# A conditioned block on one core: zero matmuls early, bias rows on another queue, and the first slot tile ahead of the second in the opening

## The chip, the core and the metric

The kernel runs on one NeuronCore of a Trainium2 chip. The core has five engines with a queue of instructions each: TensorE (PE: matmuls; its weight loads are listed apart as PEld), VectorE (DVE), ScalarE (ACT), GpSimd (POOL) and SyncE (SP), which here only starts DMAs. Sixteen DMA engines move data between HBM and SBUF, the on-chip memory; matmul results go to PSUM banks. The metric is the device time of one execution in microseconds; lower is better. The median of three runs before the change is 463.99 us.

## What is computed

`x` holds 32 sequences of 128 tokens with 512 features, all float32. `cond` holds one row of 512 per sequence, and `mask` says for each token whether it takes part in the first half of the block (for these inputs, only a minority of the tokens, at the ends of the sequences).

```python
emb = silu(t) @ ada_w + ada_b
shift, scale, gate_msa = split(emb, 3, axis=1)
norm = layernorm(x) * (1.0 + scale[:, None]) + shift[:, None]
norm = where(m, norm, 0.0)
fwd = gelu(norm @ ssm_w1 + ssm_b1) @ ssm_w2 + ssm_b2
bwd = flip(gelu(flip(norm) @ bwd_w1 + bwd_b1) @ bwd_w2 + bwd_b2)
x = x + gate_msa[:, None] * where(m, fwd + bwd, 0.0)
ff_ada = silu(t) @ ffada_w + ffada_b
shift_mlp, scale_mlp, gate_mlp = split(ff_ada, 3, axis=1)
ff_norm = layernorm(x) * (1.0 + scale_mlp[:, None]) + shift_mlp[:, None]
h = gelu_tanh(ff_norm @ ff_w1 + ff_b1)
return x + gate_mlp[:, None] * (h @ ff_w2 + ff_b2)
```

Nothing mixes tokens of a sequence, so the first half of the block has to be done only for tokens that the mask keeps.

## The kernel before

**First half: slots.** The kept tokens are packed into at most 512 slots, four tiles (0 to 3) of 128 slots; a loop at the end, not entered here, takes any remainder. The opening works out which token sits in each slot. The mask is loaded on ACT's queue (L110), counted and transposed (L427 to L441, PE result `pb`), cumulated (`pg`, L449), and combined with the slot numbers (`pick_slots`, L213). `find_slots(h)` makes, for two slot tiles at a time, one matrix product (`pl_s`, L225) and three DVE operations that end in the token indices `token_i_s`. `gather_slots` (L254) has POOL issue two indirect DMAs that fetch these rows of `x` into `xc`.

**Conditioning.** SP loads `ada_w` into `ada_a` in four blocks of rows for shift and scale (`load_ada`, L124) and one block with all rows of the gate's columns (L146). `silu(cond)` is transposed to `sT` (L460 to L466). `modulation` (L275) multiplies `sT` with `ada_a` into PSUM (`pm_ss` for shift and scale, `pm_g` for the gate, one strip of 32 output rows each) and DVE adds the bias rows `modb_a` to give `mod1`. `slot_part` (L288) turns rows of `mod1`, one per sequence, into rows per slot by a product with the 0/1 matrix `pick`. The bias rows come through `broadcast_rows` on POOL's queue (L423), three DMAs; three more on POOL's queue (L477 to L481) fetch `bias_rows`, the biases of the hidden layers.

**Slot tiles 0 and 1.** `statistics` takes both tiles at once: mean and variance of each on DVE, then one reciprocal root for both on POOL. `modulated` applies two DVE operations per tile; PE transposes each tile (`transposed_slots`, L175) into a PSUM bank and ACT copies it to `xT_s`, 256 columns for the two tiles. `hidden` (L182) then computes, for each of eight blocks f of the hidden layer, four matmuls with 256 columns into one bank (`ph_s`) and a Gelu on ACT. `project` (L196) multiplies back (`po_s`), and `finish_slots` (L296) adds the bias, multiplies by the gate, adds `xc` and stores the rows to a DRAM buffer `x1_rows`.

**Weights and queues.** SP's queue carries, in this order, the conditioning, then `w1` and `w2` (the first half's weights, in four loads), `fw1`, the conditioning of the second half `ada_f`, small bias rows, `fw2`, and the `x` of the second half. `load_behind_gathers` (L134) puts a one-element POOL memset into the target of each of the four `w` loads, so that SP issues them only after POOL has issued the gathers written ahead of them.

**Around them.** The order of the instructions on all engines is the order of the program, written out by hand (`manual_schedule`, L361). Between the first-half products, DVE also builds sums of blocks of the second half's weights (`combine`, L313, and `weight_sums`, L568), once `fw1` has landed. When tiles 0 and 1 are stored, POOL gathers their rows into the second half's `x` (`take_first_half`, L670, one indirect DMA per sequence); statistics and normalisation follow on DVE (L704 to L721), and PE transposes the result of the second group of sequences (L734) between the products of slot tile 3 (L1193). The second half runs after that, in four pairs of token groups, with block products in the manner of Strassen (`a_m`, `e_m`, L906; `a_o`, `e_o`, L1093).

**PSUM.** There are eight banks in three pools: `ps_t` (2, transposes), `ps_h` (3, hidden products), `ps_o` (3, the others). A new tile of a pool takes the bank of the oldest one and waits until its readers are done.

Of the kernel before, what the change touches and what calls it, by code (L numbers as in the profile page):

```python
# [22 lines left out]
def kernel(  # L23
# [90 lines left out]
    def broadcast_rows(t, vec, queue):  # L114

        n = vec.shape[0] // D
        each = t.shape[0] // n
        for j in range(n):
            queue.dma_start(
                t[j * each : (j + 1) * each, :],  # L120
                vec[ts(j, D)].rearrange("(o d) -> o d", o=1).to_broadcast([each, D]),
            )

    def load_ada(w, which, split):  # L124

        t = adap.tile([P, KC, 3 * D], F32, tag="ada", name=f"ada_{which}")
        for k in range(KC):
            nc.sync.dma_start(t[:, k, :split], w[ts(k, P), :split])
        return t
# [4 lines left out]
    def load_behind_gathers(t, w):  # L134
        nc.gpsimd.memset(t[0:1, 0, 0:1], 0.0)
        load_blocks(t, w)
# [7 lines left out]
    w2 = ssm.tile([P, HC, D], F32, name="w2")  # L144
    ada_a = load_ada(ada_w, "a", 2 * D)
# [227 lines left out]

    upper = ssm.tile([B, 2, 4, B], BF16, name="upper")
# [48 lines left out]
    broadcast_rows(modb_a, ada_b, nc.gpsimd)  # L423
    half = const.tile([P, G], F32, name="half")
    nc.vector.memset(half, -0.5)

# [20 lines left out]
    nc.vector.tensor_copy(maskT, pb[:, :B])  # L447
    pg = ps_t.tile([P, 512], F32, tag="tr", name="pg")
# [20 lines left out]

    token_i = find_slots(0)  # L470
    gather_slots(token_i)

    load_behind_gathers(w1[:, :, :D], ssm_w1)
    load_behind_gathers(w1[:, :, D:], bwd_w1)
    load_behind_gathers(w2[:, :KC], ssm_w2)
    load_behind_gathers(w2[:, KC:], bwd_w2)
    for key, vec in (("ssm1", ssm_b1), ("bwd1", bwd_b1), ("ff1", ff_b1)):  # L477
        n = vec.shape[0] // P
        nc.gpsimd.dma_start(
            bias_rows[col[key] : col[key] + n, :], vec.rearrange("(c p) -> c p", p=P)  # L480
        )  # L481
    pick_slots(1)
# [9 lines left out]
    modulation(pm, mod1, ada_a, modb_a, 0, 2)  # L492
    gather_slots(find_slots(1, (ps_h, "h")))
    rows = [(slot_part(c, 1, ps_o, "o"), slot_part(c, 0, ps_h, "h")) for c in range(2)]
    pm = ps_o.tile([P, 512], F32, tag="o", name="pm_g")
    xT_s = ssm.tile([P, KC, NH], F32, tag="xT", name="xT_s0", bufs=2)
    xT_t = ssm.tile([P, KC, NH], F32, tag="xT", name="xT_s1", bufs=2)
    xn = group_of_tiles("s")
    mv, rstd = statistics(xc[:2], "s01")
    xn_s = [  # L500
        modulated(
            xc[c], *rows[c], f"s{c}", xn[:, c], (mv[:, c, 0:1], rstd[:, c : c + 1])
        )
        for c in range(2)
    ]
    modulation_matmuls(pm, ada_a, 2, 3, range(KC))
# [13 lines left out]
    x_of = {0: load_x(0)}  # L520
    transposed_slots(xn_s[0], xT_s[:, :, ts(0, P)], "s0")
    transposed_slots(xn_s[1], xT_s[:, :, ts(1, P)], "s1")
# [6 lines left out]
    modulation_rows(pm, mod1, modb_a, 2, 3)  # L529

# [81 lines left out]
    for c in range(2):  # L612
        h1 += hidden(xT_s, NH, w1, 0, AF.Gelu, "s0", ssm, range(4 * c, 4 * c + 3))
        if c == 0:
            total, start_at, more_i, col_l = count_more()
        gs.append(keep_gate(c, slot_part(c, 2, ps_o, "o")))
        rows = slot_part(2 + c, 1, ps_o, "o"), slot_part(2 + c, 0, ps_o, "o")
        xn_s.append(modulated(xc[2 + c], *rows, f"s{2 + c}", xn[:, 2 + c]))
        if c == 0:
            Weights(fw1, KC // 2, FF // 2, t_1).combine(0, 1, 2, 3)  # L620
        h1 += hidden(xT_s, NH, w1, 0, AF.Gelu, "s0", ssm, range(4 * c + 3, 4 * c + 4))
        if c == 1:
            transposed_slots(xn_s[0], xT_t[:, :, ts(0, P)], "s2")
# [856 lines left out]
```

## Time and profile before

The profiled execution is one run; its span, from the first to the last instruction, is 463.6 us. The three timed runs gave 462.65, 463.99 and 466.23 us.

| | |
|---|---|
| median of three runs | 463.99 us |
| span of the profiled execution | 463.6 us |
| PE busy | 448.9 us (97%) |
| DVE busy | 330.6 us (71%) |
| first dense product (`ph_s`) starts | 20.93 us |
| bytes moved, HBM read and written | 56.83 and 13.17 MB |

How to read the profile. Times count from the start of the span, in microseconds. A row of the timeline gives the start, the length, the engine, the source line, the operation, output <- input, and how often it stands there in a row; in brackets stands how long the engine had been idle before it, and what ended that. A name with q (SPq, ACTq) is the queue that starts DMAs. PE's matmuls overlap each other: one f32 matmul of 256 columns is listed with 379 ns, but the next one starts 216 ns after it, and each f32 product appears as two instructions. A wait is put down to the event that came last. The landing of a DMA is not a row; it is seen in what waited for it, or in the list of DMAs, which gives the time from issue to landing.

### The profile page before, as it was taken

To read this page: it belongs to the slowest core of one execution; us is meant where nothing else is said; L and a number is where in the kernel's file an instruction comes from. 1 tells how busy PE (TensorE), PEld (TensorE's weight loads), DVE (VectorE), ACT (ScalarE), POOL (GpSimd) and SP (SyncE) were. 2 spreads that over 40 slices of the span, in tenths; PEclk is the share of its full clock that TensorE was granted. 3 is DMA by queue.
4 is the path that set the end of the run, shared out by engine and by line. 5 is a ranking of instruction groups with operands and counts; after the bars stand their busy time and mean duration, and the time that the engine had idled before them with its cause. 6 is when DMAs were issued, how large, how long until landed. Compare 5 with 4: busy or idle time off the path is not lost.

```text
span 463.6 us, 5827 instructions
## 1 busy us (share of the span) xinstructions
PE 448.9 (97%) x2000; PEld 364.4 (79%) x2000; DVE 330.6 (71%) x538; ACT 175.7 (38%) x380; POOL 159.8 (34%) x153
## 2 busy tenths in 40 slices
PE   6899999998999999999999999999999999999995
PEld 2475385676788888888888888888888887888884
DVE  4649778998669739996787498957963985433645
ACT  3122021743355271344455514454355144552000
POOL 6200082038981000489700005987000026560000
PEclk9999999999999999999999999999999999999998
DMA  8999836693206653923077259321872432213022
GB/s 280 386 408 364 322 107 95 219 326 104 85 5 211 97 102 105 354 90 113 1 229 113 68 169 310 99 81 34 212 105 60 155 142 79 81 74 109 0 81 105
DMA packets 82419, 70.42 MB, mean 152 GB/s; under 512 B 63168, under 2 KB 63696, under 8 KB 81362
## 3 DMA queue, kind: packets, MB, share of 16 engines
q1 hardware_dynamic: 67298, 57.03, 39.4%
q0 software_dynamic: 4480, 11.66, 7.2%
q10 hardware_dynamic: 10608, 1.32, 2.0%
q8 instruction: 17, 0.28, 0.3%
q14 instruction: 16, 0.13, 0.1%
HBM read 56.83 MB, written 13.17 MB: 151 GB/s over the span
## 4 chain that ended last, share of the span: by engine, by line
PE 72%; DVE 8%; DMA 5%; SPq 4%; POOL 4%; issue 3%; ACT 3%; POOLq 0%; ACTq 0%; DVEq 0%
PE a_o L1093 17%; PE a_m L906 14%; PE e_o L1093 13%; PE e_m L906 11%; PE ph_s L188 6%; PE po_s L203 6%; SPq L745 4%; DMA x<-in_x_dram 2%; POOL x L674 1%; DMA xc<-in_x_dram,token_i_s 1%; DMA tw<-t_rows 1%; ACT xT L728 1%; PE part_s L283 1%; POOL ha L957 1%; PE pm_f L263 1%
## 5 line engine op out<-in xcount | busy, mean ns | idle before, releaser
L957 POOL TENSOR_TENSOR ha<-p_m,ha 128x512 f32<-128x512 f32 x20 | 26.2, 1311 | 151.9 <-ACT ha L964 142.0
L1093 PE MATMUL e_o<-fw,ha 128*128 128x256 f32 x256 | 57.9, 379 | 0.0
L728 ACT ACTIVATE xT<-xT,modT 128x128 f32<-128x128 f32 x112 | 44.0, 480 | 31.9 <-DMA xT<-xn 31.9
L1093 PE MATMUL a_o<-t,hb 128*128 128x256 f32 x240 | 54.1, 379 | 0.0
L1093 PEld LDWEIGHTS e_o<-fw,ha 128*128 128x128 f32 x256 | 48.6, 190 | 6.6
L1093 PEld LDWEIGHTS a_o<-t,hb 128*128 128x128 f32 x240 | 45.6, 190 | 6.2
L674 POOL DMA_INDIRECT x<-x_rows,slot_i x32 | 38.1, 1192 | 30.1 <-DMA x_rows<-t_s 18.0
L868 ACT ACTIVATE hb<-hb,biasT 128x256 f32<-128x256 f32 x64 | 29.0, 500 | 29.1 <-POOL hb L990 19.3
L957 POOL TENSOR_TENSOR hb<-p_m,hb 128x512 f32<-128x512 f32 x20 | 29.3, 1464 | 18.9 <-DVE sx L835 18.6
L920 ACT COPY p_m<-e_m 128x512 f32<-128x512 f32 x27 | 15.8, 586 | 47.9 <-PE e_m L906 47.9
L964 ACT COPY ha<-e_m 128x512 f32<-128x512 f32 x32 | 18.5, 578 | 28.6 <-PE e_m L906 26.6
L931 DVE TENSOR_TENSOR e_m<-a_m,ha 128x512 f32<-128x512 f32 x20 | 14.0, 698 | 21.6 <-POOL ha L957 9.5
L188 PE MATMUL ph_s<-xT_s,w 128*128 128x256 f32 x128 | 28.6, 381 | 0.5 <-issue 0.5
L1093 PE MATMUL a_o<-t,s 128*128 128x256 f32 x128 | 28.9, 379 | 0.0
L1093 PE MATMUL a_o<-fw,ha 128*128 128x256 f32 x128 | 28.9, 379 | 0.0
L1093 PE MATMUL e_o<-fw,s 128*128 128x256 f32 x128 | 28.9, 379 | 0.0
L203 PE MATMUL po_s<-w,h_s 128*128 128x512 f32 x64 | 28.6, 592 | 0.0
L188 PEld LDWEIGHTS ph_s<-xT_s,w 128*128 128x128 f32 x128 | 24.0, 190 | 5.2 <-ACT h_s L192 1.5
L1093 PEld LDWEIGHTS a_o<-t,s 128*128 128x128 f32 x128 | 24.3, 190 | 3.3
L1093 PEld LDWEIGHTS e_o<-fw,s 128*128 128x128 f32 x128 | 24.3, 190 | 3.3
L1093 PEld LDWEIGHTS a_o<-fw,ha 128*128 128x128 f32 x128 | 24.3, 190 | 3.3
L868 ACT ACTIVATE ha<-e_m,biasT 128x256 f32<-128x256 f32 x48 | 20.1, 468 | 16.2 <-PE e_m L906 10.5
(210 smaller groups left out, 870.0 us busy)
## 6 DMA issues: line engine op xcount, KB each, us to landing
tw<-t_rows SPq DMA_DIRECT2D x16, 896.0 KB, 5.5
x<-in_x_dram SPq DMA_DIRECT2D x16, 512.0 KB, 6.8
gate<-gate_rows POOLq DMA_DIRECT2D x8, 1024.0 KB, 5.2
out_dram<-x SPq DMA_DIRECT2D x15, 512.0 KB, 3.3
xT<-xn SPq DMA_DIRECT2D x92, 64.0 KB, 2.4
fw<-in_L_cond_ff_w_dram SPq DMA_DIRECT2D x2, 2048.0 KB, 10.5
ada_f<-in_L_cond_ffada_w_dram SPq DMA_DIRECT2D x4, 768.0 KB, 16.7
ada_a<-in_L_cond_ada_w_dram SPq DMA_DIRECT2D x4, 512.0 KB, 6.7
```

The costliest lines, as they stand in the source:

```text
L188: nc.tensor.matmul(ph[:, :n], w[:, k, ts(f, P)], xT[:, k, :], start=(k == 0), stop=(k == KC - 1))
L203: nc.tensor.matmul(po, h[f][:, ts(i, P)], w[:, f, :], start=(f == 0), stop=(f == HC - 1))
L674: nc.gpsimd.indirect_dma_start(out=xs[i // G][i % G // 2][:, i % 2], out_offset=None, in_=x1_rows[:slots, :], in_offset=bass.IndirectOffse ...
L728: nc.scalar.activation(out, src, AF.Identity, bias=shift, scale=scale)
L745: queues[b % len(queues)].dma_start(dst[ts(q, R), b], src[ts(b, R), q])
L868: nc.scalar.activation(dst[:, n], src[:, n], AF.Gelu_apprx_tanh, bias=biasT[:, f : f + 1])
L906: nc.tensor.matmul(bank[:, ts(n, QT)], self.w_block(j, product)[:, ts(n, P)], self.x_block(j, product), start=(product in ("P1", "P5") and ...
L920: nc.scalar.copy(p5, e)
L931: nc.vector.tensor_tensor(e, a, p5, add)
L957: nc.gpsimd.tensor_tensor(self.place(RESULT[j], c), self.p5[j], other, ALU.add)
L964: nc.scalar.copy(self.place(RESULT[j], c), src)
L1093: nc.tensor.matmul(part, src[:, k, ts(i, P)], w[product][:, k, :], start=(last and k == 0), stop=True, skip_group_check=True,)
```

## The change

It touches only the opening.

1. A tile of zeros in bf16 is made first on DVE, and `keep_busy(n)` issues n matmuls of 64 columns on it into a bank that nobody reads: 36 ahead of the mask's first transpose, 4 after the products of `pb`, and 8 ahead of the first `pl_s`.
2. `modb_a` is loaded on ACT's queue, directly after the mask, instead of POOL's; `bias_rows` too, after ACT's second table load.
3. `pl_s` for slot tiles 2 and 3 stands between the second and the third block of `pm_ss` on PE, and its gathers are issued ahead of the last three `w` loads (before, all four loads came between the two pairs of gathers).
4. Each of tiles 0 and 1 has its own statistics and root. PE transposes tile 0, multiplies two blocks f with its 128 columns, transposes tile 1, multiplies a third block with tile 0's columns, and then the three blocks with tile 1's columns (`hidden_of_tile`). A bank `ph_s` collects the two halves, and one Gelu takes both. Blocks 3 to 7 are as before.
5. The gate's product `pm_g` goes to four strips of 32 rows, one per block of the sum, in place of a sum in one strip. ACT copies them to SBUF (`gate_parts`), and one more product with a 0/1 matrix `strips` (made on DVE from the identity) adds the four into `pm_gate`.

On each engine the instructions after the opening are the same, in the same order.

```diff
+    broadcast_rows(modb_a, ada_b, nc.scalar)
     ada_a = load_ada(ada_w, "a", 2 * D)
     load_blocks(ada_a[:, :, 2 * D :], ada_w[:, 2 * D :])
...
+    zeros = ssm.tile([P, P // 2], BF16, name="zeros")
+    nc.vector.memset(zeros, 0.0)
+    idle = ps_h.tile([P, 512], F32, tag="h", name="idle")
+
+    def keep_busy(n):
+
+        for _ in range(n):
+            nc.tensor.matmul(idle[: P // 2, : P // 2], zeros, zeros, start=True, stop=True)
+
+    keep_busy(36)
...
-    broadcast_rows(modb_a, ada_b, nc.gpsimd)
...
+    strips = ssm.tile([P, B], F32, name="strips")
+    nc.vector.tensor_reduce(
+        strips, ident.rearrange("p (a b) -> p b a", b=B), axis=AX.X, op=ALU.add
+    )
...
+    keep_busy(4)
     pg = ps_t.tile([P, 512], F32, tag="tr", name="pg")
...
-    token_i = find_slots(0)
-    gather_slots(token_i)
-
-    load_behind_gathers(w1[:, :, :D], ssm_w1)
-    load_behind_gathers(w1[:, :, D:], bwd_w1)
-    load_behind_gathers(w2[:, :KC], ssm_w2)
-    load_behind_gathers(w2[:, KC:], bwd_w2)
     for key, vec in (("ssm1", ssm_b1), ("bwd1", bwd_b1), ("ff1", ff_b1)):
         n = vec.shape[0] // P
-        nc.gpsimd.dma_start(
+        nc.scalar.dma_start(
             bias_rows[col[key] : col[key] + n, :], vec.rearrange("(c p) -> c p", p=P)
         )
+
+    keep_busy(8)
+    gather_slots(find_slots(0))
+    load_behind_gathers(w1[:, :, :D], ssm_w1)
     pick_slots(1)
...
-    modulation(pm, mod1, ada_a, modb_a, 0, 2)
+    modulation_matmuls(pm, ada_a, 0, 2, range(KC // 2))
     gather_slots(find_slots(1, (ps_h, "h")))
-    rows = [(slot_part(c, 1, ps_o, "o"), slot_part(c, 0, ps_h, "h")) for c in range(2)]
+    load_behind_gathers(w1[:, :, D:], bwd_w1)
+    load_behind_gathers(w2[:, :KC], ssm_w2)
+    load_behind_gathers(w2[:, KC:], bwd_w2)
+    modulation_matmuls(pm, ada_a, 0, 2, range(KC // 2, KC))
+    modulation_rows(pm, mod1, modb_a, 0, 2)
+    rows = [(slot_part(c, 1, ps_o, "o"), slot_part(c, 0, *((ps_o, "o"), (ps_h, "h"))[c])) for c in range(2)]
+    gate_parts = tp.tile([P, D], F32, tag="t", name="gate_parts")
     pm = ps_o.tile([P, 512], F32, tag="o", name="pm_g")
+    for k in range(KC):
+        nc.tensor.matmul(
+            pm[ts(k, B), :], sT[:, k, :], ada_a[:, k, ts(2, D)], start=True, stop=True
+        )
+    nc.scalar.copy(gate_parts, pm)
...
-    mv, rstd = statistics(xc[:2], "s01")
-    xn_s = [
-        modulated(
-            xc[c], *rows[c], f"s{c}", xn[:, c], (mv[:, c, 0:1], rstd[:, c : c + 1])
-        )
-        for c in range(2)
-    ]
-    modulation_matmuls(pm, ada_a, 2, 3, range(KC))
+    xn_s = [modulated(xc[c], *rows[c], f"s{c}", xn[:, c]) for c in range(2)]
...
+    def hidden_of_tile(f, c):
+
+        if c == 0:
+            ph_s[f] = ps_h.tile([P, 512], F32, tag="h", name=f"ph_s0_{f}")
+        for k in range(KC):
+            nc.tensor.matmul(
+                ph_s[f][:, ts(c, P)],
+                w1[:, k, ts(f, P)],
+                xT_s[:, k, ts(c, P)],
+                start=(c == 0 and k == 0),
+                stop=(k == KC - 1),
+                skip_group_check=True,
+            )
+
     transposed_slots(xn_s[0], xT_s[:, :, ts(0, P)], "s0")
-    transposed_slots(xn_s[1], xT_s[:, :, ts(1, P)], "s1")
+    pm = ps_o.tile([P, 512], F32, tag="o", name="pm_gate")
+    nc.tensor.matmul(pm[ts(2, B), :], strips, gate_parts, start=True, stop=True)
     ptr = ps_t.tile([P, 512], F32, tag="tr", name="ptr_b")
...
     modulation_rows(pm, mod1, modb_a, 2, 3)
+    for f in range(2):
+        hidden_of_tile(f, 0)
+    transposed_slots(xn_s[1], xT_s[:, :, ts(1, P)], "s1")
+    hidden_of_tile(2, 0)
...
     for c in range(2):
-        h1 += hidden(xT_s, NH, w1, 0, AF.Gelu, "s0", ssm, range(4 * c, 4 * c + 3))
+        if c == 0:
+            for f in range(3):
+                hidden_of_tile(f, 1)
+                t = ssm.tile([P, NH], F32, tag="h", name=f"h_s0_{f}", bufs=HC)
+                nc.scalar.activation(t, ph_s[f][:, :NH], AF.Gelu, bias=biasT[:, f : f + 1])
+                h1.append(t)
+        else:
+            h1 += hidden(xT_s, NH, w1, 0, AF.Gelu, "s0", ssm, range(4, 7))
```

More of the change, by code (lines that the diff above doesn't have):

```diff
@@ L520 @@
     x_of = {0: load_x(0)}
+    ph_s = {}
+    def hidden_of_tile(f, c):
[10 more added lines that the diff above has]
+            )
     transposed_slots(xn_s[0], xT_s[:, :, ts(0, P)], "s0")
-    transposed_slots(xn_s[1], xT_s[:, :, ts(1, P)], "s1")
+    pm = ps_o.tile([P, 512], F32, tag="o", name="pm_gate")
+    nc.tensor.matmul(pm[ts(2, B), :], strips, gate_parts, start=True, stop=True)
     ptr = ps_t.tile([P, 512], F32, tag="tr", name="ptr_b")
```

## The prediction, made before the changed kernel had run

> **What bounds the kernel now.** I read the page first (busy shares, slices, chain of waits), then the timeline of the first 90 us, then a table of stretches. PE is busy in 97% of the span, and the chain of waits is mostly PE, so the question is where PE is not yet running.
>
> ```profile
> PE 448.9 (97%) x2000; PEld 364.4 (79%) x2000; DVE 330.6 (71%) x538; ACT 175.7 (38%) x380; POOL 159.8 (34%) x153
> DMA  8999836693206653923077259321872432213022
> PE 72%; DVE 8%; DMA 5%; SPq 4%; POOL 4%; issue 3%; ACT 3%; POOLq 0%; ACTq 0%; DVEq 0%
> ```
>
> The timeline shows when dense matmuls start: the first hidden product, at 20.93. Before it one chain runs: mask, slot numbers, gather of x rows (issued 7.94, landing 14.27), statistics, modulation, transposes, copy.
>
> ```profile
> 7.94 1.05 POOL L241 DMA_INDIRECT xc<-in_x_dram,token_i_s  x1 [3.39 <-DVE inside L216]
> 14.30 0.69 DVE L155 BATCH_NORM_STATS2 st_s<-xc 128x6 f32<-128x512 f32 x1 [0.48 <-DMA xc<-in_x_dram,token_i_s]
> 20.93 5.42 PE L188 MATMUL ph_s<-xT_s,w 128*128 128x256 f32 x24 [0.49 <-issue]
> ```
>
> From there PE has no gap up to 78.65: the stretches below give it 57.72 of 57.75 us. So an opening shortened by d would shorten the kernel by d, if PE were alone. It isn't. DVE waits for the weights `fw1` until 32.82, and from then is full (20.99 of 21.80) until it has finished the second slot tile at 54.57. The store of that tile releases the gathers on POOL (57.50), whose landings hold the statistics (63.73), and so on to the four normalised tiles `xn` made at 76.92 to 78.84, which PE transposes at 78.65.
>
> ```profile
> 20.90:78.65 57.75, 57.72 (x231) 36.55 (x232) 42.77 (x80) 11.08 (x23) 14.53 (x16) 1.00 0.77 269
> 32.80:54.60 21.80, 21.80 (x81) 10.57 (x82) 20.99 (x28) 3.14 (x6) 0.55 (x1) 1.00 0.97 356
> 32.82 1.22 DVE L317 TENSOR_TENSOR t<-fw 128x1024 f32<-128x1024 f32 x1 [2.35 <-DMA fw<-in_L_cond_ff_w_dram]
> 57.50 1.11 POOL L674 DMA_INDIRECT x<-x_rows,slot_i  x1 [18.04 <-DMA x_rows<-t_s]
> 63.73 0.69 DVE L706 BATCH_NORM_STATS2 st<-x 128x6 f32<-128x512 f32 x1 [1.00 <-DMA x<-x_rows,slot_i]
> 76.92 1.92 DVE L718 TENSOR_SCALAR xn<-x,mv,rstd 128x512 f32<-128x512 f32 x4 [1.17 <-POOL rstd L712]
> 78.65 0.60 PE L734 MATMUL ptr<-ident,xn 128*128 128x128 f32 x4
> ```
>
> The first two rows are stretches: length, then busy time of PE, weight loads, DVE, ACT, POOL, then clock, DMA share, GB/s. The fourth transpose needs the last `xn` at 78.65 + 3x0.11 = 78.98, and it is ready at 76.92 + 1.92 = 78.84. **Two chains meet there with 0.14 us between them**: PE's, from the opening, and one of DMA, DVE and POOL that starts at the landing of `fw1`. PE keeps its order, so it cannot go round a late `xn`.
>
> **What the skill says.** "TensorE: Matmul & The Clock Gate", Part 1: the array runs at half rate until a window of about 3.4 us has been busy. The trace agrees: matmuls of `pm_ss` take up to 1062 ns, later ones of 512 columns 592. Part 2, LDWEIGHTS: columns / 1.2 ns, 107 for 128; the loads of the second `pl_s` stand 0.11 apart. Part 3: matmuls in different column strips run at once; `pm_f`, three strips, has its 24 instructions in 3.63 us, eight steps of 0.43. "DMA: Bandwidth & Descriptors", Issuing engines are not separate DMA queues: whichever engine issues, the same 16 DMA engines carry it; here their share is 1.01 to 1.05 from 5 to 50 us.
>
> **The change, part by part.**
>
> *Matmuls on zeros.* 36 before the mask's work, then 4 and 8. They start after the memset of `zeros`, about 1.1; the mask's transpose starts at 3.31. So a pair of load and matmul may cost 2.2/36 = 61 ns. No row shows 64 columns. The two `pt` pairs stand 0.04 apart; a cold 128-column f32 load costs 0.107 (`ptr_s`), half of that is 0.053, my value: 36x0.053 = 1.9, done at 3.0, cost 0. Bounds 0.04 and 0.107; the upper one makes the mask's chain 36x0.107 + 1.1 - 3.3 = 1.65 late. The benefit: the first `pl_s` takes 1.19 cold and 0.71 warm, so 0 to 0.5 off the gather, depending on when the clock rises. `pm_ss` gains 0.1 only: its last block of `ada_a` lands at 10.88 (DMA wait up to 10.90), and cold it was through with the others at 10.7.
>
> *Bias rows on ACT.* Three issues of `modb_a` (about 0.4 each, as SP's `modb_f` 0.33 and the mask's 0.43) go ahead of ACT's table load, so `s_sb`, done at 3.42, is done at about 4.4; its transposes (before at 4.28) come at 4.45, and with the 8 fillers `pl_s` starts near 5.4 against 5.29. Cost 0.1; if an issue takes 0.58 as on POOL, 0.6. On POOL 1.72 + 1.67 us of issue vanish, which nobody waited for except the memsets that release the weights. The bytes are the same. The three `bias_rows` issues on ACT follow the second table load, near 7, where ACT idles for 12 us; they took 5 us to land and are needed at 18. Cost 0.
>
> *Second gathers earlier.* The second `pl_s` goes between blocks 1 and 2 of `pm_ss`, so these gathers leave at 10.6 to 12 instead of 14.09. SP's second to fourth weight loads now wait behind them, until about 13.2 (before 11.05). SP has `ada_a`'s gate block (landing 14.0) and the first weights (17.56) in hand until then, so the DMAs stay full: cost 0, up to 1 if they run dry. Everything in front of `fw1` is the same bytes, so **`fw1` lands at 32.8 again**, give or take 0.3.
>
> *First tile used first.* Statistics are taken per tile: from 14.3, 0.69 + 0.18 + 0.15, then 0.74 while POOL makes the root (0.55), 0.75: `xn` of tile 0 at 16.95 (before 17.99), of tile 1 at 19.65 (19.50). `pm_g` in four strips takes 2x0.43 + 0.17 = 1.03 instead of 3.62, but its bank waits for the first modulation, so 16.2 to 17.25; its copy on ACT (0.59) ends at 17.9, the `xT_s` copy behind it at 18.5. The added `pm_gate` (2x0.43) waits for the first copy: 17.95 to 18.8, then `ptr_b` 0.17. Hidden products of tile 0 start at 19.0. A half product is 8 instructions of 128 columns at 0.108 (spacing of the warm `pl_s`) = 0.87, a whole one was 8x0.216 = 1.73: two halves cost no more. So 19.0 + 2x0.87 = 20.73; transposes of tile 1 0.44; the third half to 22.03; three halves of tile 1 to 24.65. Before, 26.35. **PE is 1.7 us ahead**; 0.6 to 2.7 with the bounds above. `strips` (0.28 on DVE, which waits for the mask until 2.95) costs 0.
>
> *What is late next.* PE reaches the transposes of `xn` at 78.65 - 1.7 = 76.95. DVE has not moved: in front of 32.82 it idles 2.3 us now and would idle 4. The second slot tile's finish needs PE's product (end 52.15), yet starts at 52.35 because DVE is busy. From `pm_f` on, DVE does get its `mod` 1.2 earlier, but the statistics still wait for gathers released at 57.50. So PE stalls about 1.6, and 0.1 is left, plus what `fw1` moves and what POOL's third gather (1.76, others 1.00) may save when DVE's sums move away from it: 0 to 0.75, taken as 0.1. Sum: 463.6 - 0.2 = 463.4 in the profiled execution's terms. The median of the runs, 463.99, is 0.4 above that span; I forecast **463.6**.
>
> **Rivals.** (a) *The lead passes through*, because `fw1` or the gathers move up with it. For: moved bias and gather traffic could let the queue move better; 118 GB/s in the second 1.5 us is spare. Against: equal bytes at a full DMA share. 463.99 - 1.7 = 462.3, down to 461.3. (b) *Slower: the fillers block PE.* PE holds the mask's transpose behind 36 pairs. At 0.21 a pair (cold spacing of `pl_s`, load and matmul) they end at 8.7, 5.4 late; less 0.5 for the clock and 1.7 for the lead leaves 3.2: 467.2. It decides from 0.11 a pair on, where lateness eats the lead. Against: the `pt` pairs. (c) *The fillers don't raise the clock*: `pm_ss` stays cold to about 10.5, the second `pl_s` inside it delays `mod1` from 12.8 to at most 14.8, still about in time for 15.4. 463.9.
>
> **Numbers.** Pinned at the transposes 0.67, (a) 0.20, (c) 0.05, (b) 0.08. The pinned case's own range is 462.8 to 464.3, runs scattering by 0.3%. The range 461.7 to 464.7 leaves out (b) and the far end of (a). One per cent is 4.6 us, about what a measurement of this kernel can tell from no change. More than the whole lead would be needed: faster 0.03, within 0.95, slower 0.02.
>
> **What would show it.** Zeros ending before 3.3, `pm_ss` at 592 ns before 10; the first hidden product near 19 and the third hidden tile done near 24.7; DVE's wait for `fw` ending at 32.8; POOL's wait for `x_rows` at 57.5; and **a new PE wait of 1 to 2 us at the L734 transposes**. If that wait is missing and the span is shorter by the lead, or if `fw` lands a microsecond from 32.8, the prediction is wrong.

## The result, and the profile after

| | before | changed |
|---|---|---|
| median of 20 runs each, side by side | 463.78 us (461.55 to 466.23) | 465.21 us (463.22 to 469.65) |
| span of the profiled execution | 463.6 us | 462.8 us (its time 464.55) |
| PE busy | 448.9 us | 450.2 us |

The ratio is 1.0036, with a 95% interval of 1.0016 to 1.0056: slower, by less than one per cent. The forecast was 463.6, and its range ended at 464.7. The two profiled spans point the other way, which is the first thing to explain. Medians and counts below leave out two executions, one of `swap` and one of `pool_queue`, that fell into a slower state.

The timeline of PE in the changed kernel shows the opening as forecast:

```profile
1.02 2.13 PE L382 MATMUL idle<-zeros 128*64 128x64 bf16 x36 [1.02 <-DVE zeros L376]
...
6.93 3.42 PE L264 MATMUL pm_ss<-ada_a,sT 128*32 128x512 f32 x8
...
18.65 2.05 PE L543 MATMUL ph_s<-xT_s,w 128*128 128x128 f32 x16
...
24.69 0.17 PE L625 MATMUL pt<-count,every 32*128 32x1 bf16 x1
...
77.58 1.60 PE L777 MATMUL ptr<-ident,xn 128*128 128x128 f32 x4 [0.35 <-DVE xn L761]
79.02 1.02 PE L204 MATMUL po_s<-w,h_s 128*128 128x512 f32 x2
...
114.67 1.13 PE L949 MATMUL e_m<-xn_sy,tw 128*128 128x256 f32 x4 [1.27 <-DVE e_m L974]
```

The zeros end at 3.15 (59 ns a pair), dense products start at 18.65, and `pt`, behind the third hidden tile, stands at 24.69 against 26.28 before: PE is 1.6 us ahead. The lead ends at the transposes of the second group. There PE waits 0.35, stretches 0.60 us of transposes to 1.60, and goes on at 79.02 (79.08 before). `pm_ss` is still cold (0.43 us an instruction), so the zeros did not raise the clock by then. The last line lies outside everything that the prediction looked at: a wait of 1.27 us at 114.67. The first profile of the kernel before, which the prediction was made from, has it too:

```profile
114.91 1.13 PE L906 MATMUL e_m<-xn_sy,tw 128*128 128x256 f32 x4 [1.26 <-DVE e_m L931]
```

So the wait alone does not tell the two kernels apart. What has to be found is where it comes from, and whether it belongs to a kernel or to an execution.

DVE, in the same execution of the changed kernel (`sx`, `hb`, `ha` and `e_m` are intermediate sums of the block products):

```profile
33.08 1.23 DVE L318 TENSOR_TENSOR t<-fw 128x1024 f32<-128x1024 f32 x1 [4.20 <-DMA fw<-in_L_cond_ff_w_dram]
...
76.88 1.92 DVE L761 TENSOR_SCALAR xn<-x,mv,rstd 128x512 f32<-128x512 f32 x4 [1.17 <-POOL rstd L755]
...
95.31 1.76 DVE L1225 TENSOR_TENSOR t_s<-t_s,xc 128x512 f32<-128x512 f32 x1
...
113.92 0.70 DVE L974 TENSOR_TENSOR e_m<-a_m,ha 128x512 f32<-128x512 f32 x1 [1.80 <-POOL ha L1000]
```

`fw1` and `xn` come when forecast. But the last operation on slot tile 3, `t_s<-t_s,xc`, takes 1.76 us where the sums of that size ahead of it take 0.68 or 0.69 (the `sx` behind it, at 97.00, takes 1.75 as well), and at 113.92 DVE has waited 1.80 us for POOL. POOL's timeline leads further:

```profile
57.95 1.08 POOL L717 DMA_INDIRECT x<-x_rows,slot_i  x1 [18.23 <-DMA x_rows<-t_s]
...
95.02 1.50 POOL L1000 TENSOR_TENSOR hb<-p_m,hb 128x512 f32<-128x512 f32 x1 [18.18 <-DVE hb L979]
...
102.48 1.12 POOL L717 DMA_INDIRECT x<-x_rows,slot_i  x1 [4.28 <-DMA x<-in_x_dram]
103.91 2.15 POOL L717 DMA_INDIRECT x<-x_rows,slot_i  x1 [0.30 <-issue]
106.36 2.08 POOL L717 DMA_INDIRECT x<-x_rows,slot_i  x1 [0.31 <-issue]
...
112.60 1.29 POOL L1000 TENSOR_TENSOR ha<-p_m,ha 128x512 f32<-128x512 f32 x1
```

POOL's sum `hb` starts at 95.02 and runs beside `t_s`. Behind `t_s`, SP stores the rows and issues four loads of `x` for the next pair. POOL waits 4.28 us for the first of these, issues six gathers, and only then, at 112.60, makes the sum `ha` that DVE, and through it PE, is waiting for.

Another execution of the kernel *before* (`b_again` below) looks like this in the same views, DVE first:

```profile
95.77 0.68 DVE L835 TENSOR_TENSOR sx<-s 128x512 f32<-128x512 f32 x1
96.37 0.69 DVE L1182 TENSOR_TENSOR t_s<-t_s,xc 128x512 f32<-128x512 f32 x1
```

```profile
96.45 1.73 POOL L957 TENSOR_TENSOR hb<-p_m,hb 128x512 f32<-128x512 f32 x1 [18.55 <-DVE sx L835]
...
102.31 1.41 POOL L674 DMA_INDIRECT x<-x_rows,slot_i  x1 [2.45 <-DMA x<-in_x_dram]
104.02 1.00 POOL L674 DMA_INDIRECT x<-x_rows,slot_i  x1 [0.30 <-issue]
...
110.90 1.27 POOL L957 TENSOR_TENSOR ha<-p_m,ha 128x512 f32<-128x512 f32 x1
```

The order of the instructions is the same; `hb` comes just after `t_s` has started instead of just before, `t_s` takes 0.69, and the gathers are through 1.7 us earlier although PE is 1.06 us *later* here (first `a_m_alone` at 88.26, in the changed kernel 87.20; part of this is TensorE's clock, which turns full at 12.0 us here and at 10.0 there). PE's waits from 85 to 130 us, in the list of waits (total, times, longest), changed kernel first:

```profile
PE e_m L949 <- DVE e_m L974: 1.6, 2, 1.3
PE e_m L949 <- DVE e_m L993: 0.9, 2, 0.4
PE a_m L949 <- ACT p_m L963: 0.7, 1, 0.7
PE a_m L949 <- DVE hb L979: 0.3, 1, 0.3
```

```profile
PE e_m L906 <- DVE e_m L931: 0.5, 1, 0.5
PE e_m L906 <- DVE e_m L950: 0.4, 1, 0.4
PE a_m L906 <- DVE hb L936: 0.3, 1, 0.3
```

That is 3.5 against 1.2 us; the first profile of the kernel before has 3.3. From the first `a_m_alone` to the first `a_o` the changed kernel needs 45.57 us, this execution 42.82. The difference of 2.75, less the lead of 1.06, is 1.69; the spans differ by 462.8 - 461.1 = 1.7.

### The profile page after: what moved, and what is told of

Read it like the earlier page. It is cut to its first block, busy times and chain, and to the rows that moved or that the text cites. A ratio compares the mean times of both kernels' runs of the same rounds, so it can differ in the third digit from the quotient of the medians.

```text
span 462.8 us, 5971 instructions
## 1 busy us (share of the span) xinstructions
PE 450.2 (97%) x2074; PEld 367.8 (79%) x2074; DVE 332.4 (72%) x541; ACT 176.3 (38%) x381; POOL 156.6 (34%) x148
## 4 chain that ended last, share of the span: by engine, by line
PE 79%; DMA 5%; DVE 5%; POOL 4%; issue 3%; ACT 1%; ACTq 0%; POOLq 0%; DVEq 0%
PE a_o L1136 23%; PE e_o L1136 18%; PE a_m L949 18%; PE e_m L949 14%; DMA b2b<-in_L_cond_bwd_b_dram 4%; POOL x L717 3%; PE po_s L204 1%; PE ph_s L543 1%; DMA xc<-in_x_dram,token_i_s 1%; PE a_m_alone L949 1%; PE last L1136 1%; POOL ha L1000 1%; DVE xn_tw L614 0%; DMA x_rows<-t_s 0%; DVE e_m L974 0%
## 5 line engine op out<-in xcount | busy, mean ns | idle before, releaser
L949 PE MATMUL a_m<-xT,tw 128*128 128x256 f32 x96 | 24.6, 379 | 0.0
L949 PE MATMUL e_m<-s,fw 128*128 128x256 f32 x92 | 23.8, 381 | 0.3 <-DVE e_m L974 0.3
```

The costliest lines, as they stand in the source:

```text
L949: nc.tensor.matmul(bank[:, ts(n, QT)], self.w_block(j, product)[:, ts(n, P)], self.x_block(j, product), start=(product in ("P1", "P5") and ...
```

## The experiments

Two theories came to stand against each other. **Theory 1:** the time is lost at 95 to 115 us, because POOL's first sum comes too early there and the `x` loads too late. **Theory 2:** it is lost in the opening, to the zeros or to a clock that rises later. The table holds what each profiled execution shows, taken from the timelines: where the bias rows are loaded; the start of the first `a_m_alone`; the length of the last `t_s`; the time from that `a_m_alone` to the first gather behind the `x` loads; the time from there to the end of the sixth gather; the time from `a_m_alone` to the first `a_o`; and the median time. The ratios are to runs of the kernel before that were taken beside each kernel; they are not exactly the quotients of the medians.

| kernel | bias | a_m_alone | t_s | to gather | gathers | to a_o | median us | ratio [95%] |
|---|---|---|---|---|---|---|---|---|
| before | POOL | 87.27 | 0.69 | 15.81 | 9.74 | 45.74 | 463.78 | |
| b_again | POOL | 88.26 | 0.69 | 14.05 | 8.56 | 42.82 | 464.25 | 1.0024 [0.9994, 1.0054] |
| early_finish_b | POOL | 87.97 | 0.68 | 13.94 | 8.66 | 42.81 | 462.86 | 0.9983 [0.9963, 1.0003] |
| only_busy | POOL | 87.96 | 0.69 | 16.53 | 10.67 | 47.37 | 464.77 | 1.0026 [1.0003, 1.0049] |
| pool_queue | POOL | 88.67 | 0.69 | 15.30 | 10.26 | 45.74 | 465.05 | 1.0009 [0.9978, 1.0041] |
| pool_early | POOL | 88.26 | 0.68 | 13.80 | 8.82 | 42.82 | 465.15 | 1.0018 [0.9997, 1.0040] |
| pool_first | POOL | 87.83 | 0.69 | 14.81 | 9.11 | 44.11 | 463.50 | 0.9993 [0.9972, 1.0015] |
| changed | ACT | 87.20 | 1.76 | 15.28 | 10.10 | 45.57 | 465.21 | 1.0036 [1.0016, 1.0056] |
| a_again | ACT | 86.72 | 1.76 | 15.39 | 9.99 | 45.56 | 466.75 | 1.0067 [1.0045, 1.0089] |
| no_busy | ACT | 87.45 | 1.76 | 15.20 | 10.18 | 45.56 | 464.44 | 1.0000 [0.9982, 1.0019] |
| early_finish | ACT | 91.05 | 1.76 | 15.11 | 10.27 | 45.57 | 465.64 | 1.0040 [1.0019, 1.0061] |
| only_queue | ACT | 86.79 | 1.76 | 15.31 | 10.06 | 45.54 | 464.67 | 1.0022 [1.0003, 1.0042] |
| swap | ACT | 87.68 | 0.68 | 14.22 | 9.52 | 43.93 | 462.10 | 0.9978 [0.9956, 1.0000] |
| swap_again | ACT | 87.79 | 0.68 | 13.98 | 8.45 | 42.63 | 462.97 | 0.9990 [0.9967, 1.0013] |
| swap_no_busy | ACT | 87.47 | 0.68 | 14.03 | 8.41 | 42.64 | 461.92 | 0.9961 [0.9939, 0.9984] |
| x_sooner | ACT | 87.73 | 0.69 | 14.28 | 9.06 | 43.53 | 462.93 | 0.9999 [0.9982, 1.0016] |
| x_sooner_b | POOL | 87.53 | 0.69 | 14.04 | 9.46 | 43.69 | 462.61 | 0.9983 [0.9963, 1.0003] |
| best | ACT | 86.43 | 0.69 | 13.50 | 8.54 | 42.25 | 462.55 | 0.9988 [0.9966, 1.0009] |
| best_again | ACT | 87.42 | 0.69 | 14.20 | 9.13 | 43.51 | 462.10 | 0.9966 [0.9948, 0.9985] |
| best_b | POOL | 87.08 | 0.69 | 14.25 | 9.25 | 43.69 | 463.75 | 1.0000 [0.9980, 1.0020] |

Medians are known to about 1 us: `b_again` is the kernel before, and its interval reaches from 0.9994 to 1.0054; the changed kernel gave 465.21 and, as `a_again`, 466.75. The stretch, the time from `a_m_alone` to `a_o`, is sharper. It is the sum of the two columns ahead of it plus 20.2 us in every row (15.28 + 10.10 + 20.19 in the changed kernel, 14.05 + 8.56 + 20.21 in `b_again`): PE's progress hangs on the end of POOL's gathers.

### First experiments: is the lead lost at the transposes, do the zeros cost

The kernel before again.

> The kernel before, unchanged, profiled a second time, to learn how typical its first trace is. Pinned theory (PE and the chain fw1 - DVE - x_rows - gathers - xn meet at the transposes of the second sequence group near 78.65): ratio 1.000; fw1's wait on DVE ends near 32.8, POOL's wait for x_rows near 57.5; the third gather (1.76 us in the first trace) is about 1.0 like the others, and xn is ready up to 0.7 earlier than 78.84. Rival (the first trace was typical in all of this): the same numbers as before to 0.1.

The changed kernel without the matmuls on zeros:

```diff
-    keep_busy(36)
...
-    keep_busy(4)
...
-    keep_busy(8)
```

> The changed kernel without the matmuls on zeros. Theory 1 (the changed kernel's 0.36% come from the DMA and DVE chain, which the fillers don't touch): ratio to the kernel before stays at 1.002 to 1.005; pl_s starts near 5.3 instead of 5.79 and the first hidden product near 18.3; the stall of PE at the transposes of xn grows to 2 us. Theory 2 (the fillers cost the time, through the clock or PE's instruction supply): ratio 0.999 to 1.001.

The finish of slot tile 1 ahead of the `fw2` sums, in the changed kernel and in the kernel before (`early_finish_b`):

```diff
     fw2_of = Weights(fw2, HC // 2, D // 2, t_2)
-    fw2_of.combine(0, 1)
...
     finish_slots(1, h1, gs[1])
...
     modulation(pm, mod2, ada_f, modb_f, 0, 3)
+    fw2_of.combine(0, 1)
```

> The changed kernel with DVE's two sums of fw2 (2.45 us) moved from ahead of the second slot tile's finish to behind the modulation of the second half, so that x_rows is stored earlier. Theory 1 (the lead of PE is lost waiting for xn, because DVE is late): the store leaves about 2.3 us earlier, xn is ready near 76.5, PE's wait of 1.6 us at these transposes is below 0.3, and the kernel is 1.5 us faster than the changed one: ratio to the kernel before 0.998 to 1.001. Rival (the end is set elsewhere, such as by the DMAs of the second half): ratio unchanged at 1.003 to 1.005.

> The same move of DVE's two fw2 sums in the kernel before. Theory 1: PE arrives at the transposes at 78.65 with or without it, so at most the 0.1 to 0.3 us of later waits are saved: ratio 0.999 to 1.000. Rival (DVE's chain alone sets the end): 2.3 us faster, ratio 0.995.

`b_again` had `fw1` at 32.82 as expected, and its third gather took 1.00 us; but the gathers started at 58.79 instead of 57.5, and the last `xn` was done at 79.86, later than in the first profile and not earlier. So the chain behind `fw1` was a microsecond later in this execution, with `fw1` in its place.

The zeros bought no time: without them the median is 0.8 us below the changed kernel's. The ratio of 1.0000 is the one of that expectation's theory 2 (the zeros cost the time), though the trace of `no_busy` has the slow `t_s` all the same. In `early_finish`, whose theory 1 had the lead kept, the median did not fall (1.0040, the rival's number); in the kernel before the same move gave 0.9983. The profiled `early_finish` has no wait at the transposes, but that says nothing about the move: PE comes there only at 82.43, as its clock rose late. (In `best`, below, which has the move and an early clock, the first transposes still take 1.40 us.) PE's timeline in `early_finish`:

```profile
16.05 3.78 PE L284 MATMUL part_s<-mod,pick 32*128 32x512 f32 x8 [0.79 <-DVE mod L274]
19.77 1.94 PE L514 MATMUL pm_g<-ada_a,sT 128*32 128x512 f32 x8
```

The same `part_s` took 1.99 and `pm_g` 1.06 in the profiled changed kernel. The recorded clock turns full at 23.0 us here and at 10.0 there. From this came theory 2. Comparing all six traces point by point gave theory 1: `t_s` takes 1.76 us in the three executions with the bias rows on ACT's queue, 0.68 or 0.69 in the three with them on POOL's.

### Second experiments: the two theories apart

The kernel before with the bias rows on ACT's queue alone (`only_queue`), the changed kernel with them on POOL's behind all loads (`pool_queue`), the kernel before with the zeros alone (`only_busy`), and `pool_early`, which is `pool_queue` with the move of `early_finish` and no zeros. The core of the first:

```diff
-    broadcast_rows(modb_a, ada_b, nc.gpsimd)
+    broadcast_rows(modb_a, ada_b, nc.scalar)
...
-        nc.gpsimd.dma_start(
+        nc.scalar.dma_start(
             bias_rows[col[key] : col[key] + n, :], vec.rearrange("(c p) -> c p", p=P)
```

> The kernel before with one part of the change alone: the bias rows are loaded on ScalarE's queue. Theory 1 (the time is lost at 95 to 115 us: the first sum on POOL of the matrix products starts 0.2 us after DVE's hb where the bias loads stand on ScalarE's queue and 0.6 us after it where they stand on POOL's, because the order of POOL's waits follows from the queues; started early it runs beside DVE's last t_s<-t_s,xc, which then takes 1.76 us for 0.69, and the x loads behind it on SP go 1.1 us later): the last t_s takes 1.7 to 1.8 us, the x loads are issued 9.9 us (not 8.8) after the first a_m_alone, the six gathers take 10 us for 8.6, PE waits 1.2 to 1.3 us for an e_m near 114, and the median is 0.8 to 2 us above the kernel before, ratio 1.002 to 1.004. Theory 2 (the time is lost in the opening, to the zeros or a later full clock): nothing moves there, ratio 0.999 to 1.001.

> The changed kernel with one part undone: the bias rows are loaded on POOL's queue again, behind the gathers. Theory 1: the last t_s<-t_s,xc takes 0.69 us again, the x loads are issued 8.8 us after the first a_m_alone, the wait of 1.3 us near 114 is gone, and the median is 462.5 to 463.6, ratio 0.997 to 0.9995, since of the lead of 1.6 us of the opening about 1 us to the first a_m stays. Theory 2: the opening stays as in the changed kernel, ratio 1.002 to 1.004.

> The kernel before with the matmuls on zeros alone (36, 4 and 8). Theory 1: PE's chain in the opening may start 0.3 to 0.6 us later, t_s and the x loads as in the kernel before, ratio 0.999 to 1.002. Theory 2: the matmuls on zeros cost what the change costs, ratio 1.002 to 1.004. If they raised TensorE's clock earlier, the matmuls of pm_ss would take about 592 ns instead of 1,062 and the ratio would be below 0.998.

> The changed kernel with three edits: bias rows on POOL's queue again, no matmuls on zeros, and the 0 and 1 sums of the second feed-forward weight moved behind the modulation of the feed-forward, so that the second slot tile's sums and its store come earlier. Theory 1: no wait of PE at the transposes of the second group and no late t_s, so the lead of the opening of 1.6 us stays: median 461.3 to 462.8, ratio 0.994 to 0.998, if the full clock comes as early as in the kernel before. Theory 2: the opening costs what it costs in the changed kernel, ratio 1.000 to 1.004.

**`only_queue` turns the slow `t_s` and the wait on by itself**, and its ratio of 1.0022, just clear of noise, is the one that theory 1 forecast. DVE's timeline in it:

```profile
94.90 1.76 DVE L1183 TENSOR_TENSOR t_s<-t_s,xc 128x512 f32<-128x512 f32 x1
```

PE waits 1.26 us at 114.25, and the stretch is 45.54 (42.82 in `b_again`, but 45.74 in the first profile of the kernel before, by another route, below). The loads are issued 10.27 us after `a_m_alone`, against 9.20 in both profiles of the kernel before (the 9.9 and 8.8 expected were those of the store ahead of them; the difference of 1.1 holds). `pool_queue` turned `t_s` back to 0.69, but was no clean undoing: its ratio of 1.0009 is above what theory 1 forecast, with an interval that holds both theories. Its recorded clock went back to half at 16.35 for 3.4 us, and its bias rows came too late for PE's `ptr_b`:

```profile
21.43 0.20 PE L556 MATMUL ptr_b<-ident,bias_rows 16*128 16x16 f32 x1 [1.15 <-DMA bias_rows<-in_L_cond_ff_b_dram]
```

and its `x` loads landed 6.1 us after their issue instead of 4.9. That second route exists in the kernel before too: with `t_s` at 0.69, the first load took 6.6 us in the profiled execution of before, 7.0 in `only_busy` and 4.6 to 4.9 in `b_again`, `early_finish_b` and `pool_early`, and the stretch follows: 45.74, 47.37, and three times 42.8. Why a load lands late wasn't found. **The medians did not decide for theory 1 alone:** `pool_early` (1.0018) and `only_busy` (1.0026) lie where theory 2 had them. In `pool_early` PE waits for the bias rows too, 1.42 us at 21.02. `only_busy` has the zeros and nothing else of the change, its `t_s` takes 0.69, and it is slower than the kernel before, just clear of noise. So the zeros have a cost of their own, which theory 1 does not account for.

### Third experiments: the loads earlier

```diff
     for j in (2, 3):
         of_x[0].one(j)
+    with_x(3)
+    x_of[1] = load_x(1, spare)
     now.do(1, "P1")
...
     now.token_sums(1, 0)
-    with_x(3)
-    x_of[1] = load_x(1, spare)
```

`with_x(3)` is the last `t_s` and its store. `x_sooner` is the changed kernel with this move, `x_sooner_b` the kernel before with it; `best` adds the move of `early_finish` and leaves the zeros out, `best_b` is the kernel before with both moves.

> The changed kernel with one move: the last t_s<-t_s,xc (DVE), its store and the four x loads (SP) stand ahead of the first product of the feed-forward instead of behind the first sum on POOL. Theory 1 (the time is lost where POOL waits for the x loads and the six gathers hold up its sums): the loads are issued at 92 to 94 us instead of 97.5, the first gather starts at 98 to 100 instead of 102.5, the waits of 1.27 and 0.45 us for e_m at 114 to 117 are gone, the median is 461 to 463 and the ratio to the kernel before 0.993 to 0.998. Theory 2 (the opening): 1.002 to 1.004 as for the changed kernel. Theory 3 (the loads take the transfer engines from tw, which lands later): a wait of PE for tw appears and the ratio stays at 1.000 or more.

> The same move in the kernel before. Theory 1: the loads no longer land too late in any execution, so the times lie closer together: median 461 to 463, ratio 0.993 to 0.998, and the changed opening alone is worth what x_sooner lies below this, 0.3 to 1.2 us. Theory 2: 0.999 to 1.001.

> The changed kernel with the x loads moved as in x_sooner, the 0 and 1 sums of the second feed-forward weight moved behind the modulation, and no matmuls on zeros. Theory 1: no wait at the transposes of the second group and none at 114, so the whole lead of the opening stays: 0.5 to 1 us below x_sooner, ratio 0.991 to 0.996. If the later full clock of the changed opening costs more than that in most executions, it is not below x_sooner.

> The kernel before with the same two moves (x loads, 0 and 1 sums). Theory 1: 0.2 to 0.4 us below x_sooner_b, and 1 to 2 us above best, which is the value of the changed opening with both losses behind it taken away. If the changed opening is worth nothing (the clock rises later in it), best is not below this one.

In `x_sooner` the wait of 1.27 us went (the one behind it fell from 0.45 to 0.33) and the stretch fell to 43.5, but not as I had thought. The loads are issued at 93.4 and land at 102.0 all the same, 8.6 us later. From 90 to 100 us the DMA share is 1.03 and 0.97, and the transfers of `tw` were issued just ahead; that these hold the loads is likely, and not shown. What the move bought is 1.0 us up to the first gather and 1.0 us in the gathers and, with these, the wait. Theory 3, a wait for `tw`, did not come. `x_sooner` lies 2.3 us below the changed kernel, yet its ratio is 0.9999, not 0.993 to 0.998, `best` is 0.4 below it with 0.9988, not 0.991 to 0.996, and `best_b` did not gain on `x_sooner_b`: differences of 1 us between medians carry little here.

### Fourth and fifth experiments: two instructions exchanged

```diff
-    now.token_sums(1, 0)
     with_x(3)
+    now.token_sums(1, 0)
     x_of[1] = load_x(1, spare)
```

That is `swap`, in the changed kernel: DVE does `t_s` just ahead of the first `sx` instead of just behind it. `pool_first` is the changed kernel with the bias rows on POOL's queue, early there: directly behind the first gathers and the first weight load. `a_again` is the changed kernel, `best_again` is `best`. `swap_again` is `swap`, taken beside `swap_no_busy`, the same without the zeros.

> The changed kernel with two neighbouring DVE instructions exchanged: the last t_s<-t_s,xc (and its store and the x loads) ahead of the first sx<-s instead of behind it. Theory 1 (POOL's first sum starts 0.2 us after DVE's hb and runs into t_s): t_s now starts before POOL does and takes about 0.7 us instead of 1.76, the x loads are issued at 95.5 to 96 instead of 97.5, the six gathers start by 101.8 and take 8.6 us, the wait of 1.27 us at 114 is gone, and the median is 1.5 to 2.5 us below the changed kernel, ratio to the kernel before 0.996 to 1.001. Theory 2 (opening): no change against the changed kernel, 1.002 to 1.004.

> The changed kernel with the bias rows on POOL's queue, where the kernel before had them, behind the first pair of gathers and the first w load. Theory 1: POOL's first sum starts 0.6 us after DVE's hb again, the last t_s takes 0.69 us, the x loads are issued 8.8 us after the first a_m_alone instead of 9.9, and the wait at 114 comes only in executions whose x loads land over 6 us after their issue: ratio 0.997 to 1.001, some executions below 463.0. Theory 2: 1.002 to 1.004.

> The changed kernel again. Both theories: ratio 1.002 to 1.005. Theory 1: the last t_s takes 1.76 us, x loads 9.9 us after the first a_m_alone, the wait of 1.27 us near 114 is there, in this execution too, and no time is below 463.0.

> The version with the x loads and the 0 and 1 sums moved and no matmuls on zeros, again. Theory 1: median 461 to 462.6, ratio to the kernel before 0.994 to 0.999, with the interval below 1, and 2 to 3.5 us below the changed kernel of the same call.

> The changed kernel with the exchange of swap, again. If the exchange takes the loss away: t_s about 0.7 us, from the first a_m_alone to the first a_o at most 44.2 us instead of 45.6, median 462 to 463.5, ratio 0.996 to 1.000.

> The same without the matmuls on zeros. If these cost time: 0.6 to 1.3 us below swap_again, ratio 0.994 to 0.998. If they cost nothing: within 0.4 us of swap_again. If they help (the clock comes earlier with them): above it by 0.5 us or more, and the first pm_ss matmuls no warmer than in swap_again.

DVE's timeline in `swap`:

```profile
94.59 0.68 DVE L979 TENSOR_TENSOR hb<-a_m_alone,p_m 128x512 f32<-128x512 f32 x1
95.19 0.68 DVE L1225 TENSOR_TENSOR t_s<-t_s,xc 128x512 f32<-128x512 f32 x1
95.79 1.77 DVE L878 TENSOR_TENSOR sx<-s 128x512 f32<-128x512 f32 x1
```

POOL's sum starts at 95.50. Now `sx`, which is next, takes the 1.77 us, and nothing is queued on SP behind it. `t_s` takes 0.68, the waits of PE from 85 to 130 us are 1.9 us instead of 3.5, and the median is 4.7 us below the changed kernel measured beside it (`a_again`, whose 1.0067 is above what both theories forecast) and 3.1 below its first measurement. The trace accounts for 45.57 - 43.93 = 1.6 of that, the one of `swap_again` for 45.57 - 42.63 = 2.9; the rest is not seen in the profiled executions.

`pool_first` confirms the other side: `t_s` 0.69, stretch 44.11, ratio 0.9993, and seven of its 22 runs are below 463.0. **The times agree with it without any trace**: of 97 runs with the bias rows on ACT's queue and `t_s` in its old place (changed, `no_busy`, `early_finish`, `only_queue`, `a_again`) none was below 463.06 us; of the 101 with `t_s` moved on top of that, 63 were; of 286 of the kernel before taken beside the experiments, 94 were. A fast `t_s` is not enough, though: with the rows on POOL's queue, `pool_queue`, `pool_early` and `only_busy` have only 7 of 57 there.

The zeros: without them the median was 1.05 us lower (`swap_no_busy` to `swap_again`), 0.8 lower in `no_busy` (against the changed kernel's own, earlier measurement), and the zeros alone made the kernel before 0.26% slower. All three agree in sign; of the two that were taken side by side, the first and the last, only the last is clear of noise. The traces show a part near the start, and then not: `pl_s` starts at 5.79 with the zeros and at 5.18 without (`no_busy`), but the first hidden product at 18.65 with them and at 18.98 without. The spans of the two profiled swaps are 460.2 and 460.3 us. So no trace shows where the cost goes; it stays open.

`swap_no_busy` (0.9961 [0.9939, 0.9984]) and `best_again` (0.9966 [0.9948, 0.9985]) are faster than the kernel before by less than half a per cent, clear of noise. `best`, which is the same kernel as `best_again`, was not (0.9988 [0.9966, 1.0009]).

## Why `t_s` gets slow

In all eleven profiled executions with the bias rows on ACT's queue POOL's sum starts 0.22 or 0.23 us after the end of DVE's `hb`, which it waits for; in all nine with them on POOL's, 0.59 or 0.60 after it. (POOL's row in `b_again` names `sx` as what ended its wait; in the program the wait on DVE is for `hb`, one instruction earlier.) In the program, engines wait for each other by semaphores, which are counters. The waits that the built program puts ahead of the sum, by what sets them, are:

```
bias on POOL:  [store of t_rows, DVE hb]  [load of b2, ACT p_m]  sum
bias on ACT:   [load of b2]  [load of bias_rows, DVE hb]  [store of t_rows, ACT p_m]  sum
```

So the queue of a small load in the opening changes on which semaphores POOL waits 90 us later, and in which grouping. That the start moves by 0.37 us with the queue is shown. That the grouping moves it is not, and the traces speak against the waits themselves: the record of the last one begins 0.08 to 0.09 us after the end of `hb` in 19 of the 20 executions, on either queue (0.46 in `pool_first`). The difference lies behind it. With the rows on ACT's queue the sum is listed 0.13 us after that record, with them on POOL's mostly 0.50, and then, in all nine, at the end of `sx` to within 0.01 us. Whether the sum is held by `sx` there, or by something else on POOL, no run separates.

What 0.37 us decide is told by the Trainium skill, "SBUF — State Buffer", section "SBUF: two separate sides": DVE and GpSimd share a pair of ports as an exclusive lock when DVE reads two inputs from SBUF and GpSimd reads SBUF too, and whichever starts first has it for its whole instruction. The trace agrees, read in this way. In `b_again`, `t_s` started at 96.37, ahead of the sum at 96.45, and took 0.69. In the changed kernel the sum was listed from 95.02, while `sx` ran until 95.40, would have come next, and ran to 96.52; `t_s`, listed from 95.31, ended at 97.07, 0.55 after it. Some DVE sum pays about 1.1 us in both orders (in `b_again` the `sx` behind `t_s`, 1.76); what matters is that behind `t_s` stand the store and the loads, and behind `sx` no DMA.

## The prediction, point by point

**What held.** Zeros at 59 ns a pair (forecast 53) ending before the mask; `pl_s` 0.5 us later, at the upper end of what was allowed; first hidden product at 18.65 (19.0), three tiles done at 24.7 (24.65), a lead of 1.6 (1.7); `fw1` at 33.08 (32.8); the gathers behind the store of the second slot tile at 57.95 (57.50); the end of the lead at the transposes, by a stretched 1.0 us instead of a wait of 1 to 2. Rival (c) was right about the clock in this execution, at no cost there. The mechanism named as likeliest happened where it was said to, in this execution: of the lead 0.07 us is left at the first `a_m_alone`, so rival (a) did not come.

**The step that failed** is "Bias rows on ACT ... Cost 0.1; if an issue takes 0.58 as on POOL, 0.6", with the issues on POOL "which nobody waited for except the memsets that release the weights". It counted the issues on both queues and looked at who needs the bytes. It did not ask what else on POOL follows from the queue: the instructions behind the opening are the same in both kernels, the waits in front of them are not, and neither is the start of POOL's sum. `only_queue` shows what that costs: the last `t_s` goes from 0.69 to 1.76, the `x` loads are issued 1.1 us later, the stretch to `a_o` is 45.54 us, against 42.8 where the loads land in time, and the ratio is 1.0022 [1.0003, 1.0042] with nothing else changed. A second term was mis-sized as well: the zeros were put at "cost 0", and `only_busy` has them at 1.0026 [1.0003, 1.0049].

**Why the sum looked right.** It was made against an execution in which the same 2.9 us were already lost, for another reason: the `x` loads had landed 6.6 us after their issue. The waits of POOL in that execution said so:

```profile
POOL x L674 <- DMA x<-in_x_dram: 4.2, 1, 4.2
```

It is the 4.3 of the changed kernel, and `b_again` has 2.4. The prediction took everything behind 79 us as fixed. Of the two profiles of the kernel before, one has the loss and one has not; of all nine with the rows on POOL's queue, three need over 45 us. With the rows on ACT's queue and `t_s` in its old place, all five need 45.54 to 45.57: a loss that comes in some executions had become one that comes in every one profiled. Against `b_again` the sum is: lead at the first `a_m_alone` -1.06, loss behind it +2.75, together +1.7. The median moved by 1.4. The step from span to median, "0.4 above that span", was wrong too: 1.75 us lie around the span in the changed kernel, so the profiled 463.6 was, by the same difference, a run near 465.4 and not a typical one. (Even as written, 463.4 and 0.4 give 463.8; the forecast of 463.6 does not follow.) With 1.75 added, the 463.4 would have met the measured 465.2. That would have been luck: the sum had the change at -0.2 us, and it came out at +1.4.

**The slower rival** had the wrong place. (b) let the zeros block the mask; they ended in time. The zeros' cost of about 1 us in the medians is on the slower side as well, but its way is not known.

**Open.** Why POOL's sum starts later with the rows on its own queue; why loads land 4.6 us after issue in one execution and 7.0 in another; why gathers take 2.1 us instead of 1.0 when they start late; where the zeros cost time; and the part of the 4.7 us of `swap` that the traces don't show.

## What to carry to other kernels

Moving a DMA to another queue moves more than its issue and its bytes: the waits ahead of later instructions on both queues can change, and with them or beside them when these start, so list waits and starts before and after the move. Where DVE and POOL both work from SBUF, put the DVE operation with DMAs queued behind it where it surely starts first. Before a sum is made against one profiled execution, profile the kernel a second time and look for waits that one execution has and the other has not, and take the chain to its end instead of to the first place where two chains meet.

## What the runs showed of the hardware, unexpected

- A 512-element two-input DVE sum took 1.76 us for 0.69 when a POOL sum had begun before it, and which of the two was hit depended on 0.4 us.
- 36 + 4 + 8 matmuls of 64 columns on zeros from 1.02 us on did not make `pm_ss` at 6.93 warm: the recorded clock turned full at 10.0 us in the changed kernel and, without them, at 10.1 in `no_busy`.
- The full clock came at 9.5 to 12.1 us in most executions, at 14.6 to 15.3 in three and at 23.0 in one (`early_finish`), though PE was busy 5.0 of 5.0 us in each of the stretches 5 to 10 and 10 to 15 there. One kernel had it at 10.5 in `best` and at 14.6 in `best_again`. The Trainium skill, "TensorE: Matmul & The Clock Gate", Part 1, says that the window of about 3.4 us runs freely and puts the spread from run to run at half a microsecond; the traces show far more.
- A wait may cost a second time. In `only_busy`, PE waited 2.55 us for the late sums, the recorded clock was at half from 116.8 for 3.4 us, and matmuls that take 1.03 us for four took up to 2.08. PE's timeline in it:

```profile
117.24 2.08 PE L918 MATMUL e_m<-xn_sy,tw 128*128 128x256 f32 x4 [2.55 <-DVE e_m L943]
119.11 1.56 PE L918 MATMUL a_m<-xn_sy,tw 128*128 128x256 f32 x4
120.51 1.03 PE L918 MATMUL e_m<-xT,fw 128*128 128x256 f32 x4
```
